# A graph block on one core: neighbour sums of projected rows, a mixer whose sums hold keys times norms, and a finer interleaving

## The chip, the core and the metric

The kernel runs on one core of one Trainium2 chip. Its engines work in parallel, each through its own list of instructions in order: TensorE (PE; weight loads are shown apart as PEld), VectorE (DVE), ScalarE (ACT), GpSimd (POOL) and SyncE (SP, which only issues DMAs here). An instruction that needs another engine's result waits on a semaphore, and everything behind it on its own engine waits too. The metric is the device time of one execution in microseconds.

## The reference

Everything starts from `xn`, the layer norm of `x` (6250 nodes of 256 channels), with 200,000 edges sorted by destination:

```python
edge_index = jnp.stack([src, dst])
xn = _layernorm(x, axis=-1)
x = x + gnn(edge_index, xn, W, b) + mix(xn[None], ...)[0]
x = x + ffn(_layernorm(x, axis=-1)[None], ...)[0]

# gnn: graph convolution with self-loops and symmetric norm
norm = dinv[src] * dinv[dst]                  # dinv = rsqrt(degree)
h = X @ W
out = segment_sum(h[src] * norm[:, None], dst) + b
return relu(out)

# mix: linear attention over all nodes (8 heads of 32), then a two-layer net
q, k = elu(q) + 1, elu(k) + 1                 # q, k, v = split(x @ Wqkv.T)
kv = einsum('nshd,nshm->nhmd', k, v);  ksum = sum(k, axis=1)
z = 1.0 / (einsum('nlhd,nhd->nlh', q, ksum) + 1e-6)
t = einsum('nlhd,nhmd,nlh->nlhm', q, kv, z)
x1 = layer_norm(t + x, ln1_g, ln1_b)
h = gelu(x1 @ W1.T + b1);  y = h @ W2.T + b2
return layer_norm(y + x1, ln2_g, ln2_b)

# ffn: each token goes to its best of 8 experts if that has room (977 tokens)
hmid = relu(buf @ w1 + b1);  ybuf = hmid @ w2 + b2
```

## The kernel before

Nodes are cut into 49 tiles of 128 rows (the last has 106), handled in 25 pairs (`twos`). The program has four stages, one after the other.

**First stage.** Two generators are interleaved by hand: for every step of `first_chain`, `FIRST` = 0.79 steps of `first_passes` are written out. `first_passes` goes over the pairs: it normalises a pair (L749), transposes it (L244), makes queries (L775) and stores them in `q_dram`, makes keys and values of each tile in one 512-wide matmul (L788), and adds keys times values to `kv_ps` (`outer`, L761; the value tile `va` has a column of ones, so that the sum of the keys comes along). ScalarE reads the bank of keys and values three times (L793 exp, L795 relu, L797 copy of the values); banks of this kind (`bank`) are three in all. `first_chain` finds where each node's edges begin (`search`), which gives the degrees and `dinv`; then it scales the rows of `xn` by `dinv` (L419), splits each into a rounded part and a remainder (L410, L412), keeps them in the SBUF table `tab` and stores them in `g_dram`; between those steps it makes the edge lists. At the end `kv_ps` is masked to the heads (L822, L823).

**Main loop.** Three generators are interleaved in a loop over j (L1353 to L1362). `gather` brings 128 source rows per step from `g_dram` by an indirect DMA (L1049) and sums them by destination with a one-hot matrix on TensorE (L1067), for 18 of the tiles, 34 steps each. `dense` makes the sums of the other 31 tiles without gathering: it builds a count matrix per tile from two small one-hots, `lo` and `hi` (L963, two buffers each), by TensorE (L1025), copies it to SBUF (L1029, L995), and multiplies it with the table (L1008); edges that fit in no list come in by one more one-hot, `ohl` (L1038, L1005). It has 352 steps. `put_sum` (L954, L955) adds the two halves of a finished sum. `rounds` takes one pair a round in each of three phases: attention and first layer norm of pair a = k+2; second layer norm and output of the mixer of pair b = k+1; and for pair c = k, whose sums must be there, the transpose (L1201), the projection by `gnn_w` (L1228), bias, relu and sum with x (L1241, L1248), the third layer norm and the logits (L1310). Every second pair, `routing` finds the expert and slot of each token and scatters the rows to `xbuf` (L1148). One yield of `rounds` comes per turn (`SIDE` = 612/612).

**Tail.** The last sums come at the end of the main loop, and the rounds that need them follow: pairs 22, 23 and 24, the last with a routing of its own.

**Experts.** For each of eight experts, its rows are loaded from `xbuf`, transposed, and go through the two layers (L1420, L1430); the result is scattered to `out` (L1448).

A branch after the first stage (L834) leads to a slow general path that these inputs do not take.

Of the kernel before, what the change touches and what calls it, by code (L numbers as in the profile page):

```python
# [18 lines left out]
P = 128  # L19
N_NODES = 6250  # L20
N_EDGES = 200000
D = 256
# [33 lines left out]
SIDE = 612.0 / NGT  # L56
NX = 6
FIRST = 0.79
# [12 lines left out]
def graph_block_kernel(  # L71
# [100 lines left out]
    wqkv_s = load_w(wqkv_t, 3 * D, "wqkv_s", raw)  # L172
# [59 lines left out]

    def bank():
        return mps.tile([P, 512], F32, name="mm", tag="mm")

    def pair(tag, bufs, name):
        return mx.tile([P, 2, D], F32, name=name, tag=tag, bufs=bufs)

# [93 lines left out]
    vas = []  # L332
    for i in range(2):
        va = raw.tile([P, 2, 129], F32, name=f"va{i}")
        V.memset(va[:, :, 128:129], 1.0)
        vas.append(va)
# [16 lines left out]
    gnn_w_s = load_w(gnn_w, D, "gnn_w_s")  # L353
# [8 lines left out]
    ln1_g_s = spread(ln1_g, wpool, "ln1_g_s")  # L362
    lb_s = spread(ln1_b, wpool, "lb_s")
# [3 lines left out]
    b2_s = spread(b2, raw, "b2_s")  # L367

    kv_ps = kps.tile([P, 2, 132], F32, name="kv_ps")
    cr_ps = rps.tile([P, 512], F32, name="cr_ps")  # L370
    sm_ps = rps.tile([P, 512], F32, name="sm_ps")
# [28 lines left out]
    def row_weights():  # L400
        w = raw.tile([P, NB], F32, name="w", tag="w")
        V.tensor_mul(w, rstd, dinv)
        nb = raw.tile([P, NB], F32, name="nb", tag="nb")
        V.scalar_tensor_tensor(nb, mv[:, :, 0], -1.0, w, op0=OP.mult, op1=OP.mult)
        return w, nb

# [7 lines left out]
    def graph_rows(t0, n, w, nb, xs, whole):  # L414


        r = rows(t0)
        for i in range(n):
            V.tensor_scalar(xs[:, i, :], xs[:, i, :], w[:r, t0 + i:t0 + i + 1], nb[:r, t0 + i:t0 + i + 1],  # L419
                            op0=OP.mult, op1=OP.add)  # L420
        if whole:
            nc.sync.dma_start(node_rows(agg, t0, n), xs)
        yield
        yield from in_parts(t0, n, xs)
        nc.sync.dma_start(node_rows(g_dram, t0, n), rows_of(t0, n).bitcast(F32))
        yield
# [13 lines left out]
    def search():  # L440
# [77 lines left out]
        rsqrt(raw, dinv, deg, 1.0, "d")  # L518
        yield
# [177 lines left out]
    def first_chain():  # L697
        yield from search()
        yield from x_stats(NB)
        w, nb = row_weights()  # L700
        lists = edge_lists()
        live = True
        again = {}

        def load_again(k):

            if k < len(twos) and 40 <= twos[k][0] < NB - 1:
                t0, n = twos[k]
                again[t0] = pair("G", 3, "xr")
                nc.sync.dma_start(again[t0], node_rows(x, t0, n))  # L710

        for k, (t0, n) in enumerate(twos):
            load_again(k + 2)
            for _ in graph_rows(t0, n, w, nb, again.get(t0, x_in(t0, n)), False):
                yield
                if live:
                    live = next(lists, "end") != "end"
        if live:
            yield from lists
        V.tensor_add(lb_s, lb_s, b2_s)  # L720
        yield from checked()
# [8 lines left out]
    def first_passes():  # L730
# [5 lines left out]
        def load(gi):  # L736
            if NX <= gi < NGR:
                t0, n = twos[gi]
                xts[gi] = pair("X", 3, "xt")
                nc.sync.dma_start(xts[gi][:rows(t0), :n, :], node_rows(x, t0, n))  # L740

        def normed(gi):
# [3 lines left out]
            xn = pair("S", 2, "xn")  # L746
            for i in range(n):
                v = xts[gi][:r, i, :] if gi >= NX else x_in(t0 + i, 1)[:, 0, :]
                nc.scalar.activation(xn[:r, i, :], v, AF.Identity,  # L749
# [9 lines left out]
        def outer(t, r, ek, va):  # L759
            for g in range(2):  # L760
                nc.tensor.matmul(kv_ps[:, g, :129], ek[:r, g * P:(g + 1) * P], va[:r, g, :],  # L761
# [742 lines left out]
```

## Time and profile before

| | before |
|---|---|
| median of 3 runs | 1711.82 us (1708.29 to 1713.45) |
| profiled execution, its own time | 1710.67 us |
| span of that execution, first to last instruction | 1708.9 us |
| mean granted TensorE clock | 0.939 of full |
| busy: PE, DVE, ACT, POOL | 1452.7, 1055.3, 902.3, 767.5 us |
| first gather issued | 294.4 us |
| last summing matmul of a gather starts | 1305.0 us |
| last scatter to `xbuf` starts | 1358.2 us |
| first expert matmul starts | 1375.2 us |

In the rows of the profile a group of instructions is named by line, engine and operation, and by output<-input tiles; then come its count, its busy time in the stretch asked for, the mean ns of one, and the idle time of the engine just before, with what ended it. A row of waits reads: waiting engine and line <- what it waited for, us in total, times, longest. A row of stretches has, after its length, the busy time of PE, PEld, DVE, ACT and POOL, then the granted clock, the DMA share and GB/s.

### The profile page before, as it was taken

The numbers are of one execution on the slowest core, as the hardware profiler recorded it, in microseconds if no ns is written. First come the engines' busy times: TensorE is split into PE (matmuls) and PEld (weight loads), VectorE is DVE, ScalarE is ACT, GpSimd is POOL, SyncE is SP. The second block draws the span as 40 slices with busy tenths as digits, with TensorE's granted clock in tenths as the row PEclk, the third lists the DMA queues.
The fourth block names the chain that finished last, engine by engine and source line by source line (L and its number), as shares of the span: only waits on it lengthen the run. The fifth ranks groups of instructions, "written<-read, shape, count | busy, mean of one in ns | idle before, by whom it ended". The sixth has DMA issues, their size and how long they took to land. (4 is left out here: it accounts for less than half of the span.)

```text
span 1708.9 us, 22695 instructions
## 1 busy us (share of the span) xinstructions
PE 1452.7 (85%) x7135; PEld 1073.5 (63%) x7135; DVE 1055.3 (62%) x3484; ACT 902.3 (53%) x2032; POOL 767.5 (45%) x776
## 2 busy tenths in 40 slices
PE   4877867889879898889888988988998289999997
PEld 1555544667667676667666766766666156777774
DVE  5767875866677777776776678767775412232322
ACT  1754554656565666576656666656664123333332
POOL 0102341766656666666666666675663101111111
PEclk9988998999989999999999999998998589999999
DMA  7635687877676767676877676766673423233330
GB/s 221 170 97 164 207 251 217 216 185 191 171 195 176 201 173 204 175 207 166 210 186 186 171 210 179 195 177 183 160 202 99 144 105 136 94 111 117 112 109 22
DMA packets 184474, 285.99 MB, mean 167 GB/s; under 512 B 27338, under 2 KB 78085, under 8 KB 184203
## 3 DMA queue, kind: packets, MB, share of 16 engines
q0 software_dynamic: 96512, 179.76, 41.0%
q1 hardware_dynamic: 87530, 103.44, 18.8%
q8 instruction: 65, 1.06, 0.3%
q10 hardware_dynamic: 288, 1.08, 0.2%
q14 instruction: 79, 0.64, 0.1%
HBM read 226.50 MB, written 60.39 MB: 168 GB/s over the span
## 5 line engine op out<-in xcount | busy, mean ns | idle before, releaser
L1049 POOL DMA_INDIRECT gt<-g_dram,idxc x612 | 612.8, 1001 | 336.6 <-PE ps L1067 201.1
L1008 PE MATMUL ps_d<-tab,A_r 128*128 128x512 f32 x1519 | 418.6, 406 | 8.0 <-ACT A_r L995 7.7
L1029 ACT CAST A<-bp 128x294 uint8<-128x294 f32 x620 | 230.1, 429 | 283.8 <-PE bp L1025 282.7
L1008 PEld LDWEIGHTS ps_d<-tab,A_r 128*128 128x128 f32 x1519 | 296.1, 196 | 77.6 <-ACT A_r L995 16.2
L1067 PE MATMUL ps<-gt,oh 128*128 128x512 f32 x612 | 261.0, 474 | 8.6 <-DMA gt<-g_dram,idxc 8.4
L1025 PE MATMUL bp<-hi,lo 128*128 128x147 bf16 x1364 | 184.5, 269 | 63.4 <-DVE hi L963 58.2
L995 ACT CAST A_r<-A 128x512 fp32r<-128x512 uint8 (+1 forms) x310 | 221.5, 721 | 6.4 <-PE ps_d L1008 5.3
L1025 PEld LDWEIGHTS <-lo 128*128 128x128 bf16 x1364 | 102.3, 108 | 163.7 <-DVE hi L963 82.5
L1448 POOL DMA_INDIRECT out<-rep,who x43 | 42.5, 988 | 303.7 <-DVE rep L1446 204.4
L963 DVE TENSOR_TENSOR lo<-rowb,two 128x512 bf16<-128x512 bf16 x341 | 142.7, 419 | 34.8 <-PE bp L1025 27.7
L1420 PE MATMUL hpf<-xet,w1e 128*128 128x512 f32 (+2 forms) x544 | 151.8, 436 | 5.7 <-ACTq L1460 3.5
L963 DVE TENSOR_TENSOR hi<-hib,two 128x592 bf16<-128x592 bf16 x341 | 156.3, 459 | 0.0
L1430 PE MATMUL ypf<-w2e,hm 128*128 128x256 f32 (+1 forms) x688 | 151.3, 379 | 0.0
L1058 DVE TENSOR_TENSOR oh<-rowb,rel 128x256 fp32r<-128x256 bf16 x306 | 127.6, 417 | 35.7 <-PE ps L1067 35.4
L1430 PEld LDWEIGHTS ypf<-w2e,hm 128*128 128x128 f32 (+1 forms) x688 | 128.9, 188 | 21.9 <-issue 3.3
L1420 PEld LDWEIGHTS hpf<-xet,w1e 128*128 128x128 f32 x544 | 85.7, 192 | 65.4 <-issue 57.5
L1067 PEld LDWEIGHTS ps<-gt,oh 128*128 128x128 f32 x612 | 112.5, 203 | 15.2 <-DMA gt<-g_dram,idxc 12.0
L1422 ACT ACTIVATE hm<-hpf,fb_s 128x512 f32<-128x512 f32 (+2 forms) x136 | 71.0, 525 | 78.6 <-PE hpf L1420 75.1
L1432 DVE TENSOR_TENSOR y<-ypf,fb_s 128x256 f32<-128x256 f32 (+1 forms) x43 | 18.2, 423 | 140.4 <-PE ypf L1430 140.4
L788 PE MATMUL mm<-wqkv_s,xnt 128*128 128x512 f32 (+1 forms) x196 | 98.7, 628 | 0.0
L1433 ACT ACTIVATE y<-y,xe 128x256 f32<-128x256 f32 (+1 forms) x43 | 21.9, 508 | 119.3 <-DVE y L1432 119.3
L1264 ACT ACTIVATE s<-s,nb,rs 128x256 f32<-128x256 f32 (+1 forms) x98 | 53.6, 597 | 52.7 <-DVE nb L1258 52.5
(342 smaller groups left out, 2114.1 us busy)
## 6 DMA issues: line engine op xcount, KB each, us to landing
g_dram<-tab SPq DMA_DIRECT2D x24, 512.0 KB
xt<-in_x SPq DMA_DIRECT2D x42, 256.0 KB
xbuf<-zeros SPq DMA_DIRECT2D x26, 384.0 KB
gt<-g_dram,idxc POOLq DMA_INDIRECT x612, 3.7
xe<-xbuf SPq DMA_DIRECT2D x8, 1028.0 KB
w1e<-in_fw SPq DMA_DIRECT2D x8, 1024.0 KB
w2e<-in_fw SPq DMA_DIRECT2D x8, 1024.0 KB
xe<-xbuf SPq DMA_DIRECT2D x8, 771.0 KB
```

The source lines that it names most:

```text
L788: nc.tensor.matmul(kp[:r, :], xnt[:, c, i * r:i * r + r], wqkv_s[:, c, D:3 * D], start=(c == 0), stop=(c == 1))
L963: V.tensor_tensor(one.rearrange("p g (w t) -> p g w t", t=2), row.rearrange("p (w t) -> p w t", t=2).unsqueeze(1).to_broadcast([P, 4, w // ...
L995: nc.scalar.copy(o[:, :s1 - s0, :], mats[u][:, s0:s1, :])
L1008: nc.tensor.matmul(acc_ps, A[:, hi - s0, :], source(hi), start=False, stop=(hi == NB - 1))
L1025: nc.tensor.matmul(both[:, :, h * GN:(h + 1) * GN], lo[:, 2 * i + h, :], hi[:, 2 * i + h, :NB * GN].rearrange("p (s k) -> p s k", k=GN), s ...
L1029: nc.scalar.copy(mats[uu][:, :, GN * g:GN * (g + 2)], both)
L1049: nc.gpsimd.indirect_dma_start(out=gt, out_offset=None, in_=g_dram, in_offset=bass.IndirectOffsetOnAxis(ap=idxs[j // P][:, j % P:j % P + 1 ...
L1058: V.tensor_tensor(oh, rowb.unsqueeze(1).to_broadcast([P, 2, P]), rel[:, m:m + 2].unsqueeze(2).to_broadcast([P, 2, P]), op=OP.is_equal)
L1067: nc.tensor.matmul(ps, ohs.pop(i), tiles.pop(i), start=False, stop=(e == EB - 1))
L1420: nc.tensor.matmul(hp[:, :nn], w1e[:, c, f * P:(f + 1) * P], xet[:, c, at:at + nn], start=(c == 0), stop=(c == 1))
L1422: nc.scalar.activation(hm[:, f, :nn], hp[:, :nn], AF.Relu, bias=fb1_s[:, e * 8 + f:e * 8 + f + 1])
L1430: nc.tensor.matmul(yp[:r, :], hm[:, f, (i - i0) * P:(i - i0) * P + r], w2e[:, f, :], start=(f == 0), stop=(f == DFF // P - 1))
```

## The change

The graph convolution is linear before its relu, so the rows are projected by `gnn_w` before they are summed: in the first stage the 512-wide matmul now makes keys and projected rows, and no values. The table rows are made from that bank by `table_row` (ScalarE scales and rounds, VectorE takes the remainder). Rows that come before `dinv` is known are kept in the place of x and finished later (`late_rows`). The mixer's sums hold keys times normalised rows (and the ones column), 257 wide; the value projection is applied once at the end, to the transposed sums. In the rounds, `take` only adds the bias to the sum (scaled by `dinv` as it leaves PSUM), and the projection is gone. The residual of the mixer's net is added by TensorE: the transposed, scaled and shifted rows that feed the first layer are multiplied with the identity into the same bank; `b2` is folded into that shift and taken back from `b1`. Each round is cut into more and smaller steps, at `SIDE` = 1.3 steps a turn, at most two, and a step that waits for sums does not count. The dense one-hots are made two steps ahead in three buffers, `ohl` earlier, and the second half of a finished sum is added one step later. The last three pairs (`TAILC` = 22) share one round and one routing of five tiles. The core of the diff:

```diff
-SIDE = 612.0 / NGT
-NX = 6
-FIRST = 0.79
+SIDE = 1.3
+XIN = 20
+FIRST = 0.8
+TAILC = 22
...
-    wqkv_s = load_w(wqkv_t, 3 * D, "wqkv_s", raw)
+    nc.sync.dma_start(wqkv_s[:, :, :2 * D], wqkv_by[:, :, :2 * D])
+    nc.sync.dma_start(wqkv_s[:, :, 2 * D:], gnn_w.rearrange("(c p) o -> p c o", p=P))
...
+    def store_rows(t0, n):
         nc.sync.dma_start(node_rows(g_dram, t0, n), rows_of(t0, n).bitcast(F32))
+    def table_row(t, h):
+        r = rows(t)
+        o = rows_of(t, 1)[:, 0, :]
+        nc.scalar.activation(o[:, :D], h, AF.Copy, scale=dinv[:r, t:t + 1])
+        V.scalar_tensor_tensor(o[:, D:], h, dinv[:r, t:t + 1], o[:, :D].bitcast(F32), op0=OP.mult, op1=OP.subtract)
+    held_back = []
+    def late_rows():
+        while held_back:
+            t0, n = held_back.pop(0)
+            for i in range(n):
+                table_row(t0 + i, x_in(t0 + i, 1)[:, 0, :])
+                yield
+            store_rows(t0, n)
...
     def first_chain():
         yield from search()
+        yield from late_rows()
         yield from x_stats(NB)
+        yield from edge_lists()
+        for g in range(2):
+            for h in range(2):
+                nc.tensor.matmul(sm_ps[:, 224 + g:225 + g], w1_s[:, h, g * P:(g + 1) * P], b2_c[:, h:h + 1],
+                                 start=(h == 0), stop=(h == 1))
+        V.tensor_tensor(b1_s, b1_s, sm_ps[:, 224:226], op=OP.subtract)
+        V.tensor_add(be1_c, be1_c, b2_c)
...
-        def outer(t, r, ek, va):
+        def outer(t, r, ek, xn):
             for g in range(2):
+                nc.tensor.matmul(kvs[g], ek[:r, g * P:(g + 1) * P], xn[:r], start=(t == 0), stop=(t == NB - 1))
...
-                nc.scalar.copy(va[:r, :, 0:128], kp[:r, D:].rearrange("p (g m) -> p g m", g=2))
+                if i == 0:
+                    direct = "dinv" in found
...
+                if direct:
+                    table_row(t0 + i, kp[:r, D:])
+                else:
+                    nc.scalar.copy(x_in(t0 + i, 1)[:, 0, :], kp[:r, D:])
...
+        V.tensor_copy(moments[:, 0, :], kvs[0])
+        nc.scalar.copy(moments[:, 1, :], kvs[1])
+        tp = bank()
         for g in range(2):
+            for h in range(2):
+                nc.tensor.transpose(tp[:, (2 * g + h) * P:(2 * g + h + 1) * P], moments[:, g, h * P:(h + 1) * P], ident)
+        nc.scalar.copy(mt.rearrange("p g h k -> p (g h k)"), tp)
+        for g in range(2):
+            kp = bank()[:, :P]
+            for h in range(2):
+                nc.tensor.matmul(kp, mt[:, g, h, :], wv_s[:, h, g * P:(g + 1) * P], start=(h == 0), stop=(h == 1))
+            V.tensor_tensor(kvb[:, g, 0:128], kp, hmask.rearrange("p a b -> p (a b)"), op=OP.mult)
...
         def put_sum(t, ps):
+            nc.scalar.activation(sums[gi][:r, t % 2, :], ps[:r, :D], AF.Copy, scale=dinv[:r, t:t + 1])
+        def put_rest(t, ps):
+            o = sums[t // 2][:r, t % 2, :]
+            V.scalar_tensor_tensor(o, ps[:r, D:], dinv[:r, t:t + 1], o, op0=OP.mult, op1=OP.add)
             there.add(t)
...
-                one = de.tile([P, 4, w], BF16, name=name, tag=name)
+                one = de.tile([P, 4, w], BF16, name=name, tag=name, bufs=3)
...
+                        if p == half - 2 and u + 1 < ND:
+                            two2 = twice(u + 1)
+                        if p < half - 1:
+                            made.append((u, p + 1, onehots(two, p + 1)))
+                        elif u + 1 < ND:
+                            two = two2
+                            made.append((u + 1, 0, onehots(two, 0)))
...
+                    if u < ND and p == half - 3:
+                        ohl = de.tile([P, P], FR, name="ohl", tag="ohl", bufs=1)
+                        V.tensor_scalar(ohl, rowb, dsub[:, DTS[u]:DTS[u] + 1], None, op0=OP.is_equal)
...
                     if u >= 1 and p == half - 1:
                         put_sum(DTS[u - 1], acc_ps)
+                        rest = DTS[u - 1], acc_ps
...
+            def take(c, first):
+                ag = sums.pop(c)
+                V.tensor_add(ag[:r, :n, :], ag[:r, :n, :], gnn_b_s[:r].unsqueeze(1).to_broadcast([r, n, D]))
+                yield
...
                     for i in range(an):
                         for g in range(2):
                             nc.tensor.matmul(yp[:ar, i, :], ht[:, g, i * ar:i * ar + ar], w2_s[:, g, :],
+                                             start=(g == 0), stop=False)
+                        for h in range(2):
+                            nc.tensor.matmul(yp[:ar, i, h * P:(h + 1) * P], x1t[:, h, i * ar:i * ar + ar], ident,
+                                             start=False, stop=(h == 1))
...
-                    V.tensor_add(s[:ar, :an, :], yp[:ar, :an, :], s[:ar, :an, :])
+                    nc.scalar.copy(s[:ar, :an, :], yp[:ar, :an, :])
...
+            batch = list(range(TAILC, NGR))
+            for c in batch:
+                while any(twos[c][0] + i not in there for i in range(twos[c][1])):
+                    yield "wait"
+                yield from take(c, at)
+            rs, nb = yield from scales()
...
+            yield from routing(batch, lgt, slots)
...
+            while alive["d"] and done_d < min(2 * j, ahead) + (n_dense - ahead) * (j + 1) / (NGT + LAG):
...
+            late = 2
+            while alive["s"] and done_s < SIDE * (j + 1) and late:
+                late -= 1
+                if step("s", S) == "wait":
+                    break
                 done_s += 1
```

## The prediction

> **What bounds the kernel now.** I read the page first, for the load of each engine.
>
> ```profile
> span 1708.9 us, 22695 instructions
> ...
> PE 1452.7 (85%) x7135; PEld 1073.5 (63%) x7135; DVE 1055.3 (62%) x3484; ACT 902.3 (53%) x2032; POOL 767.5 (45%) x776
> ...
> PEclk9988998999989999999999999998998589999999
> ```
>
> TensorE is the busiest engine by far, and its clock is not at 10 tenths in most slices. An average over the span hides that the kernel has four stages, so the second view is the busy time of each engine by stage: first passes and lists, the main loop of sums, the tail of routing, the experts.
>
> ```profile
> 0.00:294.00 294.00, 214.86 (x874) 135.90 (x875) 204.00 (x768) 142.84 (x368) 59.25 (x72) 0.92 0.62 188
> 294.00:1306.00 1012.00, 899.08 (x4816) 691.26 (x4815) 728.28 (x2361) 638.91 (x1431) 659.65 (x657) 0.95 0.72 188
> 1306.00:1375.00 69.00, 23.82 (x93) 18.30 (x93) 28.43 (x129) 12.70 (x25) 6.07 (x6) 0.61 0.37 127
> 1375.00:1708.90 333.90, 314.97 (x1354) 228.05 (x1352) 94.56 (x228) 107.81 (x211) 42.51 (x43) 0.99 0.28 97
> ```
>
> [...]The main loop is 1012 us, TensorE works 899 of them and idles 113. The experts' 334 us are not touched. So the question is what those 899 and 113 us consist of. The waits of the main loop answer for the idle part:
>
> ```profile
> POOL gt L1049 <- PE ps L1067: 201.1, 191, 5.5
> ...
> DVE ag L955 <- ACT ag L954: 60.4, 35, 4.5
> PE bp L1025 <- DVE hi L963: 49.7, 28, 4.2
> DVE z L1214 <- PE mm L1208: 44.9, 32, 3.3
> ...
> DVE s L1334 <- PE mm L1330: 43.5, 21, 3.2
> ...
> PE ps_d L1005 <- DVE ohl L1038: 33.1, 20, 4.9
> ```
>
> TensorE waits 49.7 + 33.1 = 82.8 us for one-hots from VectorE. VectorE is late not for want of time (728 of 1012 us) but because, being in order, it stood waiting itself: for ag (60.4), z (44.9), the second matmul's sum (43.5). GpSimd's gathers wait for TensorE to free their tiles, so it is behind TensorE, not ahead. The groups give the prices (the first two and the last of the main loop, the other two of the first stage):
>
> ```profile
> L1228 PE MATMUL mm<-gnn_w_s,agt 128*128 128x256 f32 x176 | 42.4, 384 | 1.4 <-ACT agt L1201 1.4
> ...
> L1208 PE MATMUL mm<-kvb,q 128*128 128x132 f32 x192 | 30.6, 284 | 1.9 <-DMA q<-q_dram 1.9
> ...
> L244 PE MATMUL mm<-ident,ag 128*128 128x128 f32 x88 | 13.7, 276 | 0.5 <-DVE ag L955 0.5
> ```
>
> ```profile
> L775 PE MATMUL mm<-xnt,wqkv_s 128*128 128x256 f32 x192 | 52.7, 423 | 1.7 <-ACT xnt L757 1.7
> ...
> L761 PE MATMUL kv_ps<-va,ek 128*128 128x129 f32 x192 | 30.5, 282 | 4.7 <-DVE ek L799 4.6
> ```
>
> An fp32 matmul of the program shows as two instructions; the busy column, not the mean, is what a group costs, since matmuls overlap.
>
> **The change part by part.** All sums are against the profiled execution: span 1708.9, its own time 1710.67, and the median of the three runs is 1711.82, 1.15 above it.
>
> *Main loop, TensorE's work.* Projecting the rows first takes out the projection of the sums (42.4) and their transposes (13.7). The residual by TensorE adds 49 tiles x 2 matmuls of 128 columns, 196 instructions like those of L1208: 196 x 30.6/192 = 31.2. Net 42.4 + 13.7 - 31.2 = 24.9 us less.
>
> *Main loop, TensorE's idle time.* The one-hot of the leftovers (ohl) is now made two steps before the tile ends; its 33.1 us should go but for about 1. The lo/hi one-hots get a third buffer and are made one step earlier (a step is 1012/352 = 2.9 us of dense work), and VectorE loses its own waits: the sum's second half (ag) is added one step after the ScalarE copy, attention is read two or more steps after its matmul, the sum on L1334 is gone, and so are the multiplications and additions of L1280, L1291 and L1334 (16.6 + 16.4 + 16.6 us). L1241 (19.1) gives way to one addition per pair, 22 x 0.69 = 15.2. VectorE's load falls from 728 to about 675. I let two thirds of the 49.7 go, 33. Together 65 us less, and 48 of the 113 stay.
>
> *Main loop, the clock.* Each long gap is followed by half clock. Twenty stretches read 0.50 to 0.51 in this loop; two of them and the sum of all:
>
> ```profile
> 471.20:478.00 6.80, 3.66 (x11) 2.76 (x12) 3.79 (x17) 0.77 (x3) 3.65 (x4) 0.50 1.05 320
> ...
> 556.50:559.90 3.40, 3.40 (x13) 2.86 (x12) 2.22 (x7) 3.40 (x9) 2.48 (x4) 0.50 1.15 352
> ...
> sum 88.60, PE 79.07 PEld 60.29 DVE 63.01 ACT 59.59 POOL 52.25; mean PE 3.95 PEld 3.01 DVE 3.15 ACT 2.98 POOL 2.61
> ```
>
> TensorE worked 79.07 us in them, at half speed: 39.5 us lost. [...] Here the stretch at 556.5 follows a gap of 3.18 us, and 18 of the 22 gaps above 2.0 us in this loop are shorter than 3.4; only four (4.89, 4.21, 4.55, 4.56) are longer. [...] I follow the trace: the stretches go with the gaps, two thirds of them, 26 us. [...]
>
> *Main loop, given back.* A gather costs GpSimd 0.942 (median) + 0.30 us before it, so 612 of them and some 44 scatters at 1.38 need 612 x 1.24 + 61 = 820 us; at a loop of about 900 it is nine tenths full. The wait for q_dram and gathered rows (8.4 now) can grow, DMA share goes from 0.72 towards 0.8. ScalarE takes over the copy of the residual sum (24 pairs x 0.59 = 14, less the 12.8 of agt) and with it the wait of up to 43.5 us that VectorE had for the same matmul; behind it queue the dense casts (L1029, L995), and for their two banks TensorE. The sum's second half waits for its ScalarE copy as before, with the one-hots behind it, and holds the dense PSUM tile a step longer; two attention banks stay held while a round waits for its sums. No row shows these at the new pace. The lower end is zero (none of it removes work, so no gain), the upper ScalarE's inherited 43.5 plus a tripled data wait, 25. I take 25 of 0 to 68, nearer to the low end because ScalarE idles 373 us of this loop. Main loop: -24.9 - 65 - 26 + 25 = -91.
>
> *First stage.* The outer products keep keys against norms, 257 columns and not 129: at L775's 52.7/192 = 0.274 against 0.159, 196 instructions cost 196 x 0.115 = 22.6 us more. TensorE idles 79 us here, 23 of them before its first matmul and 9 at the boundary; the other 47 leave room, but in the last 25 us TensorE is packed, so I count it whole. Out of VectorE's list go the scaled rows and their differences (17.5 + 16.5 us plus the last row), in come 49 table rows at 0.475 (L1241, same kind, PSUM in) = 23.3. Its 16.4 us wait (L623 for hs, nine times) shrinks with it: -12. The key bank is now freed by VectorE, whose table row waits for ScalarE's, with the next keys (L799) and so the outer product queued behind it; 0 to 49 x 2 us, taken at 5, since a bank comes round only after three allocations. ScalarE's row with a scale from memory is 0.51 (L1433) for va's 0.38: 6 us, beside 134 idle ones. SyncE's queue sees the same table stores, earlier, and the reloads of x shrink from 19 pairs and 5 to four pairs; hidden, and worth about nothing. At the end a serial chain replaces the two masks: copy 0.42, four transposes 0.6, copy 0.59, projection 1.0, mask 0.5, with handovers 4, less 1 = +3. The check's sum moves ahead of it. First stage: 22.6 - 12 + 5 + 3 = +19.
>
> *Tail.* The last sums are there at 1306, the last scatter was issued at 1358.2, behind three serial rounds. Counting yields, 832 steps stand before the last round, the loop of 619 turns at 1.3 grants 805; so 27 steps, nearly a whole mixer round and its successor, remain: 15 + 4 us by the pieces of the same round in the timeline. Then 7 us taking three pairs, 2.6 for the scales, 6 for norms and logits, 6.6 + 0.8 for one routing and five scatters at 1.3: some 50 against 54. -5, with -20 to +10 as ends.
>
> Sum: -91 + 19 - 5 = -77; 1710.7 - 77 + 1.2 = about 1635.
>
> **The rivals.** *All covers hold.* Nothing is given back and the first stage's extra work fills its idle time: main -125, first stage +5, tail -10: about 1582. For it: idle time on every other engine. Against: GpSimd at nine tenths.
>
> *The one-hots stay late.* If VectorE's lateness comes from its load in bursts and not from its waits, the 33 us and half of the 26 stay: about 1680. For it: DVE is full in some stretches (3.08 of 3.50 us from 594.0). Against: 149 us of its own waits stand in front of them.
>
> *Slower.* The key bank. Every tile's second read of the bank stands in VectorE's queue behind the list chain, whose blocks (L608 to L619) are seven instructions of 0.2 to 0.35 us, 2 us in all. TensorE has about 2.5 us of other matmuls before it needs the bank; if VectorE is later than that by 1.6 us a tile, 49 x 1.6 = 78 us eat the gain, and at 2 us it is 98: about 1730. For it: three banks, and the wait is new. Against: VectorE's load in that stage falls by 12 us.
>
> *It does not do what it says.* If the rounds at 1.3 fall behind the sums (their steps are 34.5 a pair against 1.3 x 25.3 = 33 granted), the leftover is longer: 20 us more, 1655, inside the likeliest case.
>
> **How the numbers follow.** A measurement of this kernel tells 0.3% (5 us) from no change. Likeliest case, 1605 to 1665: 0.48. All covers hold, below 1605: 0.20. One-hots late or much given back, 1665 to 1706: 0.17. No change: 0.03. Key bank, slower: 0.12. So faster 0.85. The range 1565 to 1700 leaves out the slower case and no change (0.15) and the outermost ends of two others (0.05).
>
> **What would show it.** After: the PE wait for ohl near 0 and for hi below 20; main loop near 920 us at a clock of 0.98; PE in it about 850; the outer product's group near 54 us; the first stage near 313; last scatter some 48 us after the last sum. A new wait of TensorE in the first stage for table rows on VectorE would make it wrong, and so would a main loop where TensorE waits for gathered rows.

## The result, and the profile after

The changed kernel takes 1790.3 us (median of 4 runs, 1787.47 to 1793.16), the kernel before 1712.49 beside it (four runs, 1708.29 to 1713.45): 1.0459 times as long, 95% interval 1.0435 to 1.0484. The forecast was 1635, with a range of 1565 to 1700. The change costs 78 us where 77 were to be gained.

The page of after, the lines that answer to those of before:

```profile
span 1791.3 us, 22515 instructions
...
PE 1497.8 (84%) x7053; PEld 1088.6 (61%) x7053; DVE 996.2 (56%) x3341; ACT 904.8 (51%) x2022; POOL 757.0 (42%) x776
...
PEclk9988999798898998889899889998999579999998
```

VectorE has 59 us less to do, as was meant. TensorE has 82 fewer instructions, and yet its busy time is 45 us more: about 25 of it lie in the first stage, the rest comes with the lower clock (0.91 in the loop, 0.95 before). The busy time by stage, with the same columns as before:

```profile
0.00:327.00 327.00, 240.68 (x890) 151.74 (x890) 191.37 (x741) 142.36 (x360) 55.23 (x73) 0.92 0.50 156
327.00:1380.00 1053.00, 916.24 (x4713) 688.72 (x4714) 681.90 (x2244) 639.67 (x1425) 648.02 (x650) 0.91 0.67 178
1380.00:1452.00 72.00, 22.78 (x99) 18.83 (x98) 28.41 (x131) 14.73 (x28) 11.42 (x11) 0.60 0.41 140
1452.00:1791.30 339.30, 318.07 (x1355) 229.32 (x1353) 94.48 (x228) 108.06 (x211) 42.37 (x43) 0.97 0.28 95
```

The first stage and the main loop grew, although VectorE has less to do in both and the clock of the first stage is the same. The stages to the instruction, from the same two traces (first stage: to the first gather; loop: to the last summing matmul of the gathered tiles; tail: to the first matmul of the experts):

| us | before | after | change |
|---|---|---|---|
| first stage | 294.4 | 326.2 | +31.8 |
| main loop | 1010.5 | 1061.9 | +51.4 |
| TensorE busy in it | 898.1 | 923.9 | +25.8 |
| TensorE idle in it | 112 | 138 | +26 |
| busy time in it that passes at half clock | 79.2 | 150.8 | +71.6 |
| tail | 70.2 | 64.3 | -5.9 |
| experts | 333.7 | 338.9 | +5.2 |

The waits of the loop (who waited for whom; us in all, times, longest) show where the idle time went. For ohl there is none any more, for hi 10.3 instead of 49.7. Of before and then of after:

```profile
PE ps L1067 <- DMA gt<-g_dram,idxc: 8.4, 9, 2.3
...
PE mm L1121 <- DVE fore L1117: 4.0, 2, 3.1
```

```profile
DVE six L1243 <- ACT s L1409: 34.2, 16, 5.4
...
PE ps L1131 <- DMA gt<-g_dram,idxc: 27.6, 30, 4.2
...
PE mm L1187 <- DVE fore L1183: 25.5, 11, 4.6
...
PE mm L265 <- ACT s L1257: 20.8, 17, 4.0
...
PE mm L1379 <- ACT x1t L1355: 13.2, 11, 2.0
...
PE bp L1087 <- DVE hi L1016: 10.3, 4, 7.1
```

TensorE now waits for things of the rounds: the routing's count (L1187), the first norm ahead of the transposes (L265), the transposed tile (x1t), and it waits longer for gathered rows. The statistics of the second norm wait for ScalarE's new copy of the residual sum (L1409).

One of these stalls in full, from the timelines of VectorE, ScalarE and TensorE (start, length; in brackets the idle time before):

```profile
1008.18 0.42 DVE L1243 BATCH_NORM_STATS2 six<-s 128x6 f32<-128x256 f32 x1
...
1009.57 0.37 DVE L241 TENSOR_SCALAR rs_hr<-mstat 128x6 f32<-128x6 f32 x1
...
1011.99 0.17 DVE L1298 SCALAR_TENSOR_TENSOR nb<-mstat,rs 128x6 f32<-128x6 f32 x1
1012.07 0.42 DVE L1016 TENSOR_TENSOR lo<-rowb,two 128x512 bf16<-128x512 bf16 x1
```

```profile
1006.74 0.72 ACT L1091 CAST A<-bp 128x294 uint8<-128x294 f32 x2 [0.62 <-PE bp L1087]
1012.19 1.10 ACT L1257 ACTIVATE s<-s,nb,rs 128x256 f32<-128x256 f32 x2 [4.72 <-DVE nb L1298]
```

```profile
1007.20 1.29 PE L1064 MATMUL ps_d<-tab,A_r 128*128 128x512 f32 x5
1008.33 0.51 PE L1087 MATMUL bp<-hi,lo 128*128 128x147 bf16 x4
1012.84 1.40 PE L265 MATMUL mm<-ident,s 128*128 128x128 f32 x4 [4.00 <-ACT s L1257]
```

VectorE goes through sums, attention, statistics and the reciprocal root without a pause (the root alone is eleven instructions in a row, 2.4 us). ScalarE has the norm at the head of its queue and stands 4.72 us, with the dense casts behind it; TensorE has the transposes at the head of its queue and stands 4.00 us, with the dense products behind them. ScalarE and TensorE have work, but it is queued behind a chain of VectorE's that is written out too densely.

### The profile page after: what moved, and what is told of

It is laid out like the page before. It is cut to its first block, busy times and chain, and to the rows that moved or that the text cites. A ratio compares the mean times of both kernels' runs of the same rounds, so it can differ in the third digit from the quotient of the medians.

```text
span 1791.3 us, 22515 instructions
## 1 busy us (share of the span) xinstructions
PE 1497.8 (84%) x7053; PEld 1088.6 (61%) x7053; DVE 996.2 (56%) x3341; ACT 904.8 (51%) x2022; POOL 757.0 (42%) x776
## 5 line engine op out<-in xcount | busy, mean ns | idle before, releaser
L1110 POOL DMA_INDIRECT gt<-g_dram,idxc x612 | 605.7, 990 | 367.8 <-PE ps L1131 221.1
L1064 PE MATMUL ps_d<-tab,A_r 128*128 128x512 f32 x1519 | 430.1, 415 | 8.7 <-ACT A_r L1047 8.6
L1064 PEld LDWEIGHTS ps_d<-tab,A_r 128*128 128x128 f32 x1519 | 303.0, 201 | 83.3 <-ACT A_r L1047 18.0
L1131 PE MATMUL ps<-gt,oh 128*128 128x512 f32 x612 | 258.5, 472 | 38.1 <-DMA gt<-g_dram,idxc 27.6
L1087 PE MATMUL bp<-hi,lo 128*128 128x147 bf16 x1364 | 187.6, 271 | 15.9 <-DVE hi L1016 10.3
L1524 PE MATMUL hpf<-xet,w1e 128*128 128x512 f32 (+2 forms) x544 | 154.6, 442 | 8.0 <-ACTq L1564 3.5
L1131 PEld LDWEIGHTS ps<-gt,oh 128*128 128x128 f32 x612 | 112.4, 206 | 52.1 <-DMA gt<-g_dram,idxc 25.1
L1524 PEld LDWEIGHTS hpf<-xet,w1e 128*128 128x128 f32 x544 | 86.8, 194 | 69.6 <-issue 62.5
L1214 POOL DMA_INDIRECT xbuf<-slot,put x49 | 54.5, 1113 | 86.1 <-issue 71.0
```

Of the source, the lines that this page charges most:

```text
L1064: nc.tensor.matmul(acc_ps, A[:, hi - s0, :], source(hi), start=False, stop=(hi == NB - 1))
L1087: nc.tensor.matmul(both[:, :, h * GN:(h + 1) * GN], lo[:, 2 * i + h, :], hi[:, 2 * i + h, :NB * GN].rearrange("p (s k) -> p s k", k=GN), s ...
L1110: nc.gpsimd.indirect_dma_start(out=gt, out_offset=None, in_=g_dram, in_offset=bass.IndirectOffsetOnAxis(ap=idxs[j // P][:, j % P:j % P + 1 ...
L1131: nc.tensor.matmul(ps, ohs.pop(i), tiles.pop(i), start=False, stop=(e == EB - 1))
L1524: nc.tensor.matmul(hp[:, :nn], w1e[:, c, f * P:(f + 1) * P], xet[:, c, at:at + nn], start=(c == 0), stop=(c == 1))
```

## The experiments

The runs stand on several chips. On some of them before takes 1710 to 1712 us, on two others 1837 and 1839; every ratio is to before on the same chip, and stages are compared only between chips where before takes the same.

**First four kernels.** The suspicion was the finer steps, and separately VectorE's second half of the table row. e1 takes the dense part's edits (third buffers, one-hots a step earlier, ohl early, the sum's second half a step later) into before, e2 merges the finer steps, e3 gives the rounds more steps, e4 moves one instruction. (e1 reads the first norm's scale and shift from the tiles of the second, so its output is not the reference's; it has as many instructions in the rounds as before.)

```
e1, in before:  one = de.tile([P, 4, w], BF16, name=name, tag=name, bufs=3)   and put_rest, made, ohl as in after
e2, in after:   -SIDE = 1.3  +SIDE = 1.0      some ten yields inside take, the statistics and scales() removed
e3, in after:   -SIDE = 1.3  +SIDE = 1.7
e4, in after, table_row split in two:
     nc.scalar.activation(o[:, :D], h, AF.Copy, scale=dinv[:r, t:t + 1])
-    V.scalar_tensor_tensor(o[:, D:], h, dinv..., o[:, :D]..., op0=OP.mult, op1=OP.subtract)
...
     V.scalar_tensor_tensor(ek[:r], ek[:r], 1.0, rk[:r], op0=OP.min, op1=OP.add)
+    if direct:
+        table_rest(t0 + i, kp[:r, D:])
```

> The kernel before with only the edits to the sums: one-hots two steps ahead in three buffers, the leftovers' one-hot made earlier, the second half of a sum added one step later (to make room, the first norm's scale and shift in the residual are those of the second norm; the instructions are as many as before). Pacing theory (the loss in the main loop comes from the rounds' steps, which stand too close together at 1.3 a turn): these edits are good by themselves, the main loop falls from 1011 us to 910 to 960 and the whole to 1610 to 1660. Rival (the one-hots ahead themselves do the harm, since VectorE now stands in front of full buffers with the rounds' work behind it): main loop 1011 or longer, whole 1710 or more.

> The changed kernel with the rounds' steps merged back to about 18 a round and one step a turn (still at most two, and a wait still not counted). Pacing theory: TensorE's waits for the norms, for the first layer's input and for the routing's sums shrink by more than half, half-clock stretches fall from 29 to below 20, and the main loop falls from 1062 us to 960 to 1010. Rival (one-hots ahead): no change, 1050 to 1070. Rival (the residual on TensorE and ScalarE's copy of it): no change either, since both stay.

> The changed kernel with SIDE 1.7 for 1.3: the rounds' steps come faster still. Pacing theory: dependent steps stand 1.3 times closer, main loop longer by 10 to 40 us (1070 to 1100). Rivals: within 5 us of 1062, or shorter because the rounds end earlier.

> The changed kernel, with VectorE's half of each table row written out one step later, behind the next keys' instruction. Theory for the first stage: VectorE stands 50 us in front of ScalarE's half of the row, and the list chain behind it makes TensorE wait 26 us for hs; then hs falls to below 15 us and the first gather is issued 8 to 20 us earlier than 326. Rival (the wider outer product is all of it): 326 within 4 us.

Measured, beside a before of 1711.77: e1 1667.45 (0.9747, 0.9701 to 0.9793), e2 1888.54 (1.1018, 1.0966 to 1.1069), e3 1805.12 and e4 1752.75 (one run each).

e1 shortens the loop to 964.4: the dense edits are worth 46 us by themselves, so the loss of after's loop comes from the other edits. e4 brings the first gather from 326.2 to 291.5 us and TensorE's wait for hs from 24.6 to 7.9. The waits of the first stage, of after and then of e4:

```profile
DVE tab L435 <- ACT tab L434: 53.8, 28, 3.8
...
PE et_ps L644 <- DVE hs L640: 24.6, 12, 3.3
```

```profile
PE et_ps L650 <- DVE hs L646: 7.9, 8, 2.4
...
DVE tab L440 <- ACT tab L434: 4.7, 7, 1.0
```

In after VectorE stood 53.8 us in front of ScalarE's half of the row, with the edge lists behind it. One step later the half is there. With 291.5 the stage is even shorter than before's, so what the outer product of twice the width costs is hidden, or paid for by what the change takes out of this stage; no run parts the two.

e2 and e3 were to separate steps that are too coarse from steps that are too close; both made the loop longer. e3's 24 us are what the pacing theory had said; e2, which was to be 50 to 100 us shorter, is 108 longer, and the theory that the steps' size was to blame fell. e17 below offers a reading of the two: in each, as in after, a turn in which a round waits is not counted, and the rounds then go on at two steps a turn. Counted out of the program's own loop, two steps fall on 299 of 661 turns in after, on 420 of 634 in e3, and on 285 of 629 in e2, where a step is also larger. In e2 a further 302 turns have none, against 100 in after: the rounds stand and run by turns.

**Four edits on e4**, on a chip where before takes 1836.62 us. One run each.

```
e5:  e2's merged steps, waiting turns counted (the break on "wait" removed), late = 1
e6:  -    stat(s[:ar, i, :], ar, 2 + i)         +    stat(yp[:ar, i, :], ar, 2 + i)
e7:  -    late = 2                              +    late = 1 + j % 2
e8:  -    ..., tag=name, bufs=3)                +    ..., tag=name)      and the one-hots one step ahead, as before
```

> The changed kernel with the later remainder, with the merged steps of the coarse run, and with a wait counted as a step and one step a turn at most, as in the kernel before: a round that has waited for its sums does not catch up. Burst theory (VectorE's work of a round, about 11 us from taking the sums to the scales, is pressed into half the turns when rounds catch up at two a turn after a wait; TensorE then overtakes it): loop falls from 1056 us (and from 1170 with merged steps) to 940 to 1000, waits of TensorE for the first norm below 40 us. Rival (the residual's extra hop through ScalarE, DVE six <- ACT s, is what makes merged steps slow): loop stays above 1060.

> The changed kernel with the later remainder; the second norm's statistics read the bank where TensorE left the residual sum, not ScalarE's copy of it. Hop theory: the 34 us that VectorE waits for that copy fall below 15, and the loop falls from 1056 us by 15 to 40. Burst theory: loop within 12 us of 1056.

> The changed kernel with the later remainder; at most one and two steps in alternate turns, so that catching up after a wait goes at 1.5 steps a turn and not 2. Burst theory: fewer half-clock stretches than 26 and the loop 10 to 35 us below 1056. Rivals: within 8 us of it.

> The changed kernel with the later remainder; the dense one-hots go back to one step ahead in two buffers, the rest of the dense edits stays. Burst theory: the waits for the norms turn back in part into waits for hi, loop 1056 to 1085. Rival (the one-hots ahead put VectorE behind full buffers and make the loss): loop falls by 20 us or more, to 1035 or less.

Measured: e5 1818.32, e6 1872.84, e7 1843.19, e8 1865.15. e4 itself was not run here; e9, which is e4 on a chip with a before of 1838.6, took 1857.28. Against before these are 0.990, 1.020, 1.004, 1.016 and 1.010. So e5, which never takes two steps in a turn, stands 2% below e4; a second step in every other turn only (e7, still 259 such turns) stands 0.7% below it, reading the bank instead of ScalarE's copy (e6) 1% above it, and e8's half a per cent is too little to tell. Chips of like speed are not one chip and each kernel ran once, so all four are hints only; and the loop times that were forecast, counted from e4's 1056 us, do not apply on a chip where the same loop takes 1156.

**Old steps and residual**, on the chip with a before of 1838.6.

```
e10, in e4, the whole generator rounds as in before, but:
-    tp = turn(ag, cr, cn) ... hp = ... gnn_w_s ...        (transpose and projection of the sums)
+    V.tensor_add(ag[:cr, :cn, :], ag[:cr, :cn, :], gnn_b_s...)
-    V.tensor_add(s..., yp..., s...)
+    ident products into yp, nc.scalar.copy(s..., yp...), yield
-SIDE = 1.3    +SIDE = 1.0        while c is not None and ...: yield   (counted)

e11, in e1: the last three edits of the residual as in e10
e12, in e4: -done_d < min(2 * j, ahead) + ...    +done_d * (NGT + LAG) < n_dense * (j + 1)
```

> The kernel of e4 (after, with VectorE's half of the table row one step later) once more, as the base that the next three share a chip with. Nothing is changed against e4: about 1752 us beside a kernel before of 1712, and first gathering DMA near 292 us, loop near 1056 us. If the kernel before is longer than 1712 here, its own stages say by how much the chip stretches them.

> e9 with the rounds' steps as they were before: sums, attention, statistics and norms in the old order and under the old yields (waiting turns counted, one step a turn, every pair of tiles in a round of its own), while the graph rows stay projected, the residual stays on TensorE with ScalarE's copy, and the gatherers' and dense part's edits stay. Theory 'the steps': the main loop falls by 60 to 95 us against e9, to 960 to 1000, and the total to 1650 to 1690; the waits for the first norm, for the routing's counts and for gathered rows go back to about 10 us each. Theory 'the residual and its copy': the loop stays within 15 us of e9's, since the copy and the identity products are still there.

> The kernel before with the dense part's edits of e1 and, added to them, the residual by TensorE (identity products into yp, ScalarE's copy to s one step ahead of the statistics, b2 put into the first norm's shift and taken out of b1). The whole computation is there, unlike in e1. TensorE gets 25 times 4 products more (about 25 x 0.8 = 20 us of its time if all of it shows), VectorE loses three passes over a pair a round (about 25 x 2 = 50 us of its time). Theory 'the steps': the loop is within 20 us of e1's 964, the total 1655 to 1690, which would beat both kernels. Theory 'the residual': the loop is 30 to 60 us longer than e1's and the total 1700 to 1730.

> e9 with the dense part's steps spread evenly over the turns, as before, and not eleven steps ahead of it. In the trace of after the first summing matmul of the gathered tiles comes 21 us after the first gather (before: 7) and the first twentieth of the loop takes 8 us longer as well. Theory 'the lead is only shifted work': those 20 us come back, but each later twentieth gets about 0.8 us longer and the loop is within 8 us of e9's. Theory 'the lead costs': the loop is 12 to 25 us shorter.

Measured: e9 1857.28; e10 1796.21 (0.9773, 0.9732 to 0.9814); e11 1855.42 (1.0106, 1.0058 to 1.0155); e12 1854.93. With the old steps the loop goes from 1155.7 to 1094.6 us, 61 less, although the residual stays: the steps (their order, their size and how they catch up, together) cost that much. The dense part's lead (e12) is only shifted work, 4.5 us of the loop. What e11 costs against e1 can't be read across two chips; against e10, on the same chip, it is 59 us longer, and the main difference is that its rows are not projected first.

**Dense edits, residual, rows, on one chip** with a before of 1710.66.

```
e14, in e10:
+    V.tensor_mul(s..., s..., ln1_g_s...)      V.tensor_add(s..., s..., lb_s...)
-    nc.tensor.matmul(yp[...], x1t[...], ident, start=False, stop=(h == 1))
-    nc.scalar.copy(s[:ar, :an, :], yp[:ar, :an, :])
+    V.tensor_add(s[:ar, :an, :], yp[:ar, :an, :], s[:ar, :an, :])
```

> The kernel of e1 once more (before with the dense part's edits alone; the first norm's scale and shift are again read from the second's tiles, which leaves the times as they are and the output not the reference's), to stand on one chip with the next three. On the first chip it was 0.975 of before. Theory 'the dense edits are good everywhere': 0.97 to 0.98 of before here too. Theory 'they only filled gaps that the first chip had': 0.99 to 1.01 on a chip where before takes 1839 us.

> e10 (projected rows, dense part's edits, the rounds' old steps) with the residual back on VectorE: no identity products into yp, no ScalarE copy, instead the multiplication by ln1_g, the addition of the shift and the addition of yp that before had; the whole computation is there. TensorE has 192 products fewer in the loop (21 us in e4's trace), ScalarE 24 copies of 0.6 us, VectorE about 50 us more. Theory 'the residual cost, because TensorE is the bound': 15 to 35 us shorter than e15, and the shortest of the four, 0.955 to 0.97 of before. Theory 'the residual helped, because VectorE's bursts end what TensorE waits for': 10 to 40 us longer than e15.

> The kernel of e10 once more, unchanged, so that e13, e14 and e16 stand beside it on one chip: 0.973 to 0.982 of before where before takes 1839 us; about 0.99 of before, near 1695, where it takes 1712 (e4 was 1.024 of before there, less e10's 3.3%).

> The kernel before, unchanged, for its trace on this chip: within 0.3% of the other runs of before in this call. If they take about 1839 us, the loop is some 110 to 125 us longer than the 1010.5 of its first trace and first stage, tail and experts are within 5 us of theirs; then the chip stretches the loop alone, by stretches at half clock and by idle time of TensorE that no other engine explains.

Measured: e13 1672.43 (0.9784, 0.9747 to 0.9822), e14 1653.14 (0.9666, 0.9642 to 0.9691), e15 1684.39 (0.9854, 0.9825 to 0.9883), e16 1703.91. **e14 beats both kernels.** (e13, like e1, leaves out the first norm's own scale and shift. Before is no slower on this chip, so e16 only repeats its stages, with a loop of 1006.5 us for 1010.5, and what e13 would do on a slower chip stays untested.) The busy time of the whole loop, of e15 and then of e14:

```profile
291.50:1275.80 984.30, 884.84 (x4743) 672.49 (x4742) 683.78 (x2264) 644.37 (x1429) 663.62 (x655) 0.95 0.72 192
```

```profile
292.10:1253.30 961.20, 864.13 (x4550) 651.63 (x4549) 727.16 (x2336) 630.71 (x1405) 667.17 (x655) 0.95 0.74 196
```

With the residual back on VectorE, that engine works 43 us more, TensorE 20.7 less, and the loop is 23.1 shorter. TensorE's idle time is the same (99 and 97). So moving the residual to TensorE costs what its products take, and takes off VectorE nothing that was on the path once the one-hots have their lead. (The other 10 of the 31 us lie in the experts, whose code is the same; the last section says where.)

Against e13, e14 has the projected rows: TensorE works 32 us less in the loop (864.1 for 896.4), but the loop is only 8.3 shorter. The waits of e13 and of e14:

```profile
PE ps L1079 <- DMA gt<-g_dram,idxc: 12.7, 12, 3.7
```

```profile
PE ps L1137 <- DMA gt<-g_dram,idxc: 34.4, 34, 3.2
PE ps_d L1070 <- ACT A_r L1053: 15.2, 22, 4.8
PE mm L265 <- ACT s L1326: 14.9, 16, 2.4
```

Twenty-two of the 32 us went into waiting for gathered rows (27.6 us in after already). The prediction named this wait, and gave as its reason a GpSimd that is nine tenths full. That reason is not shown: in the loop of e14 GpSimd works 667 of 961 us and stands 140 us because TensorE has not freed the tiles it gathers into:

```profile
POOL gt L1116 <- PE ps L1137: 140.3, 181, 6.4
```

**Bunching, and the gathers' lead**, with a before of 1709.6.

```
e17, in e14: while c is not None and any(...):
-        yield
+        yield "wait"          (not counted; then up to two steps a turn, as in after)
e18, in e14: -LAG = 7    +LAG = 8
```

> e14 (0.967 of before, loop 961) with one edit: a turn in which a round waits for its sums does not count as a step and, as in after, up to two steps are taken in one turn until the rounds have caught up. In e14 every turn has one step at most; here 287 of 655 turns have two, as in after (299 of 661). All instructions and their order within a round stay. Theory 'the bunching': the loop gets 25 to 60 us longer, with waits of TensorE for the first norm, the routing's counts or gathered rows; 0.98 to 1.0 of before. Theory 'the order and the finer steps': within 10 us of e14, 0.962 to 0.973 of before, as the instructions come in the same order on each engine within a round.

> e14 with the gathers' lead raised from seven turns to eight (nine buffers as before). TensorE waits 34.4 us for gathered rows in e14, in 34 waits of 1 us. Theory 'the rows come late': a turn more is about 1.6 us, so most of the 34 waits go and the loop is 10 to 30 us shorter, total near 1630 to 1645 where before takes 1711. Theory 'the buffers bound them': with eight of nine buffers in flight a gather is issued only when TensorE has freed the buffer of the turn before, the rows come no earlier, and the loop is within 8 us of e14's or longer.

Measured: e17 1812.92 (1.0611, 1.0588 to 1.0635), e18 1668.51 (0.9755, 0.9727 to 0.9783).

e17 has e14's instructions, in e14's order within the rounds, and is 160 us longer, the loop 1122.7 instead of 961.2. Nothing was changed but when the rounds' steps come, that is, how they fall between those of the gatherers and the dense part. Its waits:

```profile
ACT s L1326 <- DVE nb L1320: 124.5, 23, 7.2
...
PE mm L265 <- ACT s L1326: 77.1, 16, 6.4
...
PE mm L265 <- DVE lo L1022: 42.6, 7, 6.4
...
PE mm L1193 <- DVE fore L1189: 31.6, 11, 3.8
```

And the first and the last of these in e14:

```profile
ACT s L1326 <- DVE nb L1320: 37.9, 17, 3.8
...
PE mm L1193 <- DVE fore L1189: 3.2, 10, 0.6
```

The same chain as in the timeline of after: VectorE's root, ScalarE's norm, TensorE's transposes. TensorE waited 14.9 us for the norm in e14. With two steps in a turn, half as much dense and gathered work stands between a producer and its consumer, and ScalarE and TensorE stand behind it. Counted out of the loop, 287 of e17's 655 turns have two steps and 318 none, where after has 299 and 100 of 661: e17 bunches more, in larger steps, which fits its greater loss. In e17 the rounds also run closer behind their sums, and no run parts this from the two steps; but the long waits lie inside the rounds, behind VectorE's statistics and root. The order of the steps is not needed to explain it, and the prior expectation that bunching would cost 25 to 60 us was too small.

e18: one turn more of lead leaves the wait for rows where it was (34.7) and adds 11 us of waiting for ag (25.2 for 14.2); the loop is 14 longer. That fits the theory that nine buffers bound the lead; more buffers weren't tried.

The way from after to e14, all where before takes 1710 to 1713 us:

| kernel | us | first stage | loop | TensorE busy, idle in it | what is different |
|---|---|---|---|---|---|
| after | 1790.3 | 326.2 | 1061.9 | 923.9, 138 | |
| e4 | 1752.75 | 291.5 | 1055.7 | 916.4, 139 | VectorE's remainder a step later |
| e15 | 1684.39 | 291.5 | 984.3 | 884.8, 99 | old steps, waits counted, never two in a turn |
| e14 | 1653.14 | 292.1 | 961.2 | 864.1, 97 | residual on VectorE |
| e17 | 1812.92 | 290.2 | 1122.7 | 918.5, 204 | e14 with two steps a turn after a wait |

After with the catching up taken out and nothing else was not run. From e4 to e15 the order of the steps, their size and the catching up change together, 71 us of loop. That catching up by itself can cost more than this is shown by e17; how it shares the 71 us with the other two stays open.

## Why the prediction was wrong

The stages add up: +31.8 + 51.4 - 5.9 + 5.2 = 82.5, and the two spans differ by 82.4. Step by step:

- *TensorE's work, -24.9.* In full-clock time (busy less half of what passed at half clock, an estimate: five dense products in a row take 1.29 us at 457.34 in after, and 2.33 at 1022.69, where the clock reads 0.50) it fell from 858.5 to 848.5, by 10. The direction is right. The residual's products add 21.3 us, not 31.2 (the time by which each ends after the one before it, in the loop of after), but other groups grew where they stand alone behind a wait: the transposes of s and slot from 25.1 to 36.5 by the same measure. What came out is 48.7 by it, not 56.1, so the net of these three terms, 27.4, is near the forecast.
- *Idle time, -65.* The mechanism was right and a little better than told: the waits for ohl and hi fell by 33.1 + 39.4 = 72.5.
- *Given back, +25 of 0 to 68. This is the step that failed.* Idle time rose by 26 although 72.5 had gone, so 98 came back, beyond the upper end. Two of the places were named (gathered rows +19, and ScalarE's copy, which holds up VectorE for 34.2), but the bulk of TensorE's new waits, some 60 us, was not looked for: norms, x1t and the routing's counts, all of them short waits inside the rounds. The prediction counted the yields to find out whether the rounds end in time (832 against 805), and did not ask in which turns they fall. It took more steps a turn as a gain in pace; e17 shows them to be a loss in distance, 160 us there.
- *The clock, -26.* It went the other way, as the idle time did: 29 stretches at half clock instead of 20, with 150.86 us of work in them instead of 79.07, an estimated 36 us lost on top (half of the difference). The sum over those stretches in after:

```profile
sum 177.50, PE 150.86 PEld 111.63 DVE 109.38 ACT 82.00 POOL 73.47; mean PE 5.20 PEld 3.85 DVE 3.77 ACT 2.83 POOL 2.53
```

Main loop: +51 where -91 was forecast. Work at half clock is most where TensorE idles most (83.1 us of it beside 97 idle in e14, 79.2 beside 112 in before, 150.8 beside 138 in after, 185.7 beside 204 in e17), but it does not go one for one with the long gaps. In before's loop 19 of the 22 gaps over 2.0 us have a stretch at half clock that begins in them or within 2 us of their end; the other three, of 2.26, 3.08 and 3.08 us, have none, and the clock reads 1.00 for the 20 us after each of them. In after's loop nine of the 29 stretches have no gap over 2.0 us in the 4 us before them: the one at 463.1 comes behind gaps of 1.85 and 1.22 us close together, the one at 377.8 behind a single gap of 3.03. Here two short waits stood before half clock as one long one did. The 26 us were an estimate from the long gaps; what decides which gaps half clock follows is not shown.

- *First stage, +19.* The outer products cost 23.1 us more of TensorE's time (47.5 for 24.4, by the time each ends after the one before it; all but four are in the two groups below) against the 22.6, but e4 shows a stage no longer than before with them in it; the relief of 12 for hs turned into 8 more; and the term of the key bank, taken at 5, held the whole of it: VectorE in front of ScalarE's half of the row, about 35 by e4. The rival that ended slower named this very queue, VectorE's second read with the lists behind it, at 78 to 98 us. It was real, at less than half its price, and it was not what decided.

```profile
L770 PE MATMUL kv_ps<-s,ek 128*128 128x257 f32 x128 | 35.2, 400 | 1.1 <-DVE ek L815 0.8
L770 PE MATMUL kv_ps<-xn,ek 128*128 128x257 f32 x64 | 17.1, 390 | 0.2 <-DVE ek L815 0.2
```

- *Tail, -5.* It is -5.9, and the last scatter comes 50.2 us after the last sum, where 48 were said.
- *Experts, 0.* They take 5.2 more, by one stop of TensorE at a branch and the half clock with it (last section).
- *What would show it.* Right: no wait for ohl, hi below 20, the outer products near 54 (52.3 and four more instructions, 2.1). Wrong: the loop near 920 at a clock of 0.98 (1062 at 0.91) and the first stage near 313. Of the two signs named as making it wrong, gathered rows came as told, and the table row came one link further back: VectorE waits for its first half, and TensorE for the hs behind it.
- *The rival that rounds at 1.3 fall behind* was put down as a matter of 20 us in the tail, inside the likeliest case. Pace was the right subject; its place was the loop.
- *The rival that all covers hold* has -125 for the loop; without the 25 given back the terms above make -116. Nothing hangs on it.

e14 leaves out the finer steps, the catching up and the residual by TensorE, and keeps the projected rows and the dense edits. It gains 58 of the 77 us that were forecast, by another sum: the dense edits alone bring 38 (e13) and the projected rows 19 more. Between the traces of e13 and e14, 22 us apart, 8 lie in the loop, 5 in the tail and 7 in the experts, whose code is the same. In the loop a good part of what they save on TensorE is lost to gathered rows.

## What to carry to other kernels

Where several strands are woven by hand into in-order queues, a strand that has fallen behind must not catch up in bunches: the work of the others between a producer and its consumer is what hides the latency, and with two steps a turn there is half of it (160 us of 1653 here, without one instruction changed). Ask of each new instruction on a shared queue what stands behind it and whether its input is there at its turn; a step later can be free (one moved line brought some 35 us). And do not unload an engine that is not the bound onto the one that is: VectorE's 43 us were worth nothing, TensorE's 21 cost 23.

## What was not expected of the hardware

The same program runs the loop at different speeds on different chips. e4 and e9 are one kernel: the loop takes 1055.7 us on one chip and 1155.7 on the other, first stage (291.5, 296.3), experts (338.8, 338.5) and the single instruction being nearly the same (the cast to A_r 720 and 719 ns, the one-hot hi 461 and 460). On the slow one TensorE stands for nothing that the profile shows:

```profile
PE bp L1095 <- issue: 49.6, 32, 6.4
PE bp L1095 <- ACT A L1099: 34.9, 27, 6.4
...
PE mm L265 <- issue: 12.0, 10, 3.9
```

The trace of e4 has no wait for "issue" in the loop (in e9 they are 74 us in all), and only 6.1 us for A. Work at half clock goes from 137.0 to 206.1 us. What stops TensorE there is open; it changes how kernels rank (e10 is 0.977 of before there, the same kernel as e15 0.985 elsewhere), so a comparison needs its base on the same chip.

The experts' code is the same in all kernels, and yet its stage takes 332.5 to 343.4 us. It goes with the kernel and not with the run: 333.7 and 332.5 in two traces of before, 341.4 and 342.4 in e10 and e15, 338.8 and 338.5 in e4 and e9. The traces show where it lies: at the branch that asks whether an expert has more than 512 rows. In e15 (first row) TensorE stands there twice for some 3 us, in e14 (second row) for less than 1:

```profile
PE hpf L1489 <- PEq L1527: 6.4, 2, 3.3
```

```profile
PE hpf L1486 <- ACTq L1524: 1.4, 2, 0.7
```

TensorE has no gap over 2 us in this stage in before, e8, e14, e16, e17 and e18, and the stage takes 332.5 to 334.4 us; one, at this branch, in after, e1, e3, e4, e7, e9 and e13, and 336.8 to 339.4; two in e2, e5, e6, e10, e11, e12 and e15, and 340.9 to 343.4. With each stop comes a stretch at half clock of 3.4 or 6.8 us (in after a stop of 3.0 us, L1524 <- PEq L1562, and 6.8 us at 0.50 from 1749.9). Why the branch stops TensorE in some kernels and hardly in others, no run here shows.
